# A chunk's sums are added to X by GpSimd, and the last output goes in two pieces

## The chip, the cores and the metric

The kernel runs on one core of a Trainium2 chip. A core has five engines with a queue each[...]: TensorE (PE in the profile, with its weight loads as PEld), VectorE (DVE), ScalarE (ACT), GpSimd (POOL) and SyncE (SP, which here only starts DMA transfers). The metric is the device time of one execution in microseconds (us), the median of several.

## The reference

A residual network of four layers on x of shape (4, 32, 32, 16): batch, height, width, channels. Each layer normalizes x by group norm (8 groups) and adds its result to x.

```python
def _L0_conv_ref(inputs, M, W, G):
    first = jnp.einsum('ijyx,byxc->bijc', Msq, inputs)
    kern = jnp.transpose(G, (0, 1, 5, 4, 2, 3)).reshape(h * w * f, c, G.shape[2], G.shape[3])
    shifted = lax.conv_general_dilated(x_nchw, kern, STRIDES, PADDING)
    ...
    diff = jax.nn.relu(inputs[:, None, None, :, :, :] - shifted)
    second = L * jnp.einsum('ijyx,bijyxc->bijc', Wsq, diff)
    return first - second

    x = x + _L0_conv_ref(_gn(x), L0_conv_M, L0_conv_W, L0_conv_G)
    x = x + _L1_conv_ref(_gn(x), L1_conv_M, L1_conv_W, L1_conv_G)
    x = x + _L2_conv_ref(_gn(x), L2_conv_W0, L2_conv_b0, L2_conv_W1, L2_conv_b1, L2_conv_W2, L2_conv_b2)
    x = x + _L3_conv_ref(_gn(x), L3_conv_M, L3_conv_Wp, L3_conv_G)
```

Layers 0, 1 and 3 are such convolutions. Each of the 1024 output positions has 3x3 filters of its own (G), which are applied to the whole image; the difference to the image, cut by a relu, is summed over the image with the weights W. Layer 2 is an interval layer: running maxima over intervals, then two steps with a maximum over split points and a sigmoid.

## The kernel before

The batch is cut in two groups g of two images. Three convolutions for two groups make six phases, in the order (g0, first), (g1, first), (g0, second), (g1, second), (g0, third), (g1, third), numbered 0 to 5. `X[g]` holds the group's x in SBUF as 128 partitions x 8 chunks x 32 (two images by 16 channels).

A phase runs over 8 chunks t of 128 output positions, a chunk over 32 steps (f, b): 16 channels by two images. A step is one bank pair of PSUM (`pc`, 128 x 1024), of which there are four. `first_part` (L588) writes products with the weights WU and WL and lets ScalarE scale the bank (L609); `second_part` (L612) adds the products with WD and W9, and VectorE then multiplies the bank, cut at zero, by the chunk's weights `WT` and sums it into one column of `acc` (L625, output `junk`, which nobody reads). TensorE runs one step ahead: the first part of a step is issued before the second part of the step in front of it. With the last of the 32 steps, VectorE adds the chunk's 32 sums, scaled by 1/EPS, to `X[g][:, t]` (L639). In the order of the instructions this stands behind the next chunk's first `first_part`.

Beside the steps two generators hand out small pieces of other work. `prep_parts` (L193) makes the weights: a unit is 4 channels of a chunk, 190 units in all are made here, one per 8 steps, two units ahead of their use. For a unit, VectorE cuts off the low bits (`upper`, L177), ScalarE makes W9, WD and WU (L153, L210, L213), GpSimd adds and subtracts (L223, twice L225, L187 for the next unit, twice L214), and then SP loads the raw weights of a later unit (`load_raw`, L98). `behind` (L670) prepares the next phase's images: group norm (L275), whose first sum (L279) reads all of `X[g]` of the group of the next phase, then transposes and DMAs through DRAM, then splitting of the images, on GpSimd too (L254, L261). In phases 3 and 4 it also computes the interval layer (L440): memsets (L453), a selection (L472), scans on VectorE (L483), products (L504, L517), and in two calls of `step` (L526) eight tables each on GpSimd (L536), each followed six steps later by a maximum over it on VectorE (L543).

All queues are in order: an instruction that waits for a semaphore holds all behind it on its engine. The schedule is the order in which the program is written; no scheduler moves anything. At the end SP writes `out[1]` from `X[1]` when the last chunk has been added (L841); `out[0]` went earlier, in phase 5 (L693).

Of the kernel before, what the change touches and what calls it, by code (L numbers as in the profile page):

```python
# [12 lines left out]
ALU = mybir.AluOpType  # L13
# [9 lines left out]
NT = NP // P  # L23
# [10 lines left out]
EPS = 2.0**-12  # L34
# [7 lines left out]
def net_kernel(ctx: ExitStack, tc: tile.TileContext, x, xq, xi, convs, iv_w, iv_b, out):  # L42
# [21 lines left out]
    nc = tc.nc  # L64
# [17 lines left out]
    phases = [(g, layer) for layer in range(NL) for g in range(NG)]  # L82
    n_chunks = len(phases) * NT

    X = [const.tile([P, NT, GC], F32, name=f"X{g}") for g in range(NG)]
# [487 lines left out]
    def products(ps, pairs, first):  # L573


        for k, (w, v) in enumerate(pairs):
            for h in range(2):
                r = slice(64 * h, 64 * h + 64)
                nc.tensor.matmul(  # L579
                    ps[:, h, :],  # L580
                    lhsT=w[r],
                    rhs=v[r],
                    start=first and k == 0,
                    stop=k == len(pairs) - 1,
                    skip_group_check=not first,
                )
# [25 lines left out]
    def second_part(step, ps):  # L612

        phase, t, f, b = step
        g = phases[phase][0]
        n = phase * NT + t
        u = n * NU + f // FU
        if u >= PLAIN:
            WU, WL, WD, W9 = (w[..., f % FU, :] for w in units[u])
            products(  # L620
                ps, [(WD[:, s], iyz[g][:, s, b]) for s in range(2)] + [(W9, im9[g][:, b])], False
            )
        col = b * C + f
        junk = work.tile([P, NP], F32, tag="junk", name=f"junk_{n}_{col}")
        nc.vector.scalar_tensor_tensor(  # L625
            junk,
            ps.rearrange("p h n -> p (h n)"),
            0.0,
            chunks[n],
            op0=ALU.min,  # L630
            op1=ALU.mult,
            accum_out=accs[phase][:, t, col : col + 1],
        )
        if (f, b) == (C - 1, GB - 1):
            acc = accs[phase][:, t]
            if n == 0:
                plain_acc = acc.rearrange("p (b c) -> p b c", c=C)[:, :, : PLAIN * FU]
                nc.vector.tensor_scalar_mul(plain_acc, plain_acc, EPS)
            nc.vector.scalar_tensor_tensor(  # L639
                X[g][:, t], acc, 1.0 / EPS, X[g][:, t], op0=ALU.mult, op1=ALU.add  # L640
            )

    accs = {}
    open_steps = []
# [1 line left out]
    def conv_layer(phase, behind):  # L646


        kind, wait = 1, 0
        accs[phase] = work.tile([P, NT, GC], F32, tag="acc", bufs=2, name=f"acc_{phase}")  # L650
        for t in range(NT):
            n = phase * NT + t
            steps = [(f, b) for f in range(C) for b in range(GB)]
            if n == 0:
                steps.sort(key=lambda s: (s[0] // FU, s[1]))
            for at, (f, b) in enumerate(steps):
                may = next(parts, (IDLE, CALM)) if n or at >= FIRST else (IDLE, CALM)
                if at == 4:
                    load_chunk(n + 1)
                step = (phase, t, f, b)  # L660
                open_steps.append((step, first_part(step)))
                if len(open_steps) > 1:
                    second_part(*open_steps.pop(0))
                wait -= 1
                if wait <= 0 and (kind > 0 or kind in may):
                    kind = wait = next(behind, 1 << 20)
        for _ in behind:
            pass
# [169 lines left out]
    for phase in range(len(phases)):  # L838
        conv_layer(phase, behind(phase))
    second_part(*open_steps.pop(0))  # L840
    nc.sync.dma_start(out[1], X[1])  # L841


# [74 lines left out]
```

## Time and profile before

| | us |
|---|---|
| median of 3 runs | 2578.73 (2576.74 to 2578.93) |
| the profiled execution | 2578.01 |
| its span | 2576.30 |
| L625 on VectorE, 1536 times | 1223 ns each |
| L214, L225, L223 on GpSimd, 950 times | 1303 to 1314 ns each |
| L639 on VectorE, 48 times | 24.3 in sum, 507 ns each in the mean |
| GpSimd idle before L223, waiting for ScalarE's W (L153) | 814.5 in sum, at most 13.0 |
| `out` from X, 128 KB, from issue to landing | 1.7 (the last) and 2.0 |

The profile is that of one execution. Lines of the order of time give the start in us from the span's start, the length in us, engine, line, operation, and the tiles written and read; in square brackets stands how long the engine was idle before it and what ended that. In the list of waits stand the sum, the number and the longest. Ends of matmuls are modelled, so TensorE's losses are better read from the spacing of starts. One step takes TensorE about 1.63 us, a chunk about 52.3.

### The profile page before, as it was taken

What the parts mean: (1) busy time and instruction counts of PE and PEld (TensorE: products, weight loads), DVE (VectorE), ACT (ScalarE), POOL (GpSimd) and SP (SyncE); (2) the same over time, 40 slices, a digit from 0 to 9 for tenths busy, and PEclk for the clock granted to TensorE, in tenths of its full rate; (3) what the DMA queues carried; (4) which work ended last, traced back from release to release, by engine and by line L of the source; (5) the groups of instructions that cost most, each with busy time, mean ns of one, the idle gap of its engine ahead of it and who ended that gap; (6) DMA issues with size and microseconds to landing.
All of it is one profiled execution on the core that took longest, in us unless ns stands there. A gap on an engine that the chain in (4) does not pass through costs nothing.

```text
span 2576.3 us, 56475 instructions
## 1 busy us (share of the span) xinstructions
PE 2558.4 (99%) x21906; PEld 2058.9 (80%) x21906; DVE 2150.0 (83%) x3651; ACT 2094.3 (81%) x2549; POOL 1565.7 (61%) x1289
## 2 busy tenths in 40 slices
PE   8999999999999999999999999999999999999999
PEld 5998788878888887888887877877778877788887
DVE  9888778888787887787789988889889887787777
ACT  4888788888888887888888888888888888788886
POOL 4667455575555556555566776576767676455553
PEclk9999999999999999999999999999999999999999
DMA  4424222242222432222222222322222234222220
GB/s 153 167 81 129 75 91 99 82 128 91 91 99 87 149 114 91 98 91 85 85 94 91 91 93 84 120 91 91 91 91 85 93 119 156 76 99 91 91 91 19
DMA packets 50284, 254.14 MB, mean 99 GB/s; under 512 B 12128, under 2 KB 14048, under 8 KB 24928
## 3 DMA queue, kind: packets, MB, share of 16 engines
q1 hardware_dynamic: 49056, 249.94, 28.9%
q8 instruction: 172, 2.82, 0.4%
q14 instruction: 96, 0.79, 0.1%
q10 hardware_dynamic: 832, 0.58, 0.1%
q0 software_dynamic: 128, 0.02, 0.0%
HBM read 248.99 MB, written 0.98 MB: 97 GB/s over the span
## 4 chain that ended last, share of the span: by engine, by line
PE 97%; DVE 2%; issue 1%; ACT 0%; DMA 0%; DVEq 0%; ACTq 0%
PE pc L579 96%; DVE junk L625 1%; PE pf L381 1%; ACT pc L609 0%; PE ps_l L504 0%; DMA XQ<-in_xq 0%; DVE s_a L543 0%; DVE s_b L543 0%; PE ps_r L517 0%; DVE X L639 0%; ACT L547 0%; ACT L319 0%; ACT s_a L547 0%; PE ps_y L565 0%; DVE raw L786 0%
## 5 line engine op out<-in xcount | busy, mean ns | idle before, releaser
L625 DVE SCALAR_TENSOR_TENSOR junk<-pc,WT 128x1024 f32<-128x1024 f32 x1536 | 1879.2, 1223 | 401.3 <-PE pc L579 351.3
L609 ACT ACTIVATE pc<-pc 128x1024 f32<-128x1024 f32 x1520 | 1531.6, 1008 | 445.6 <-PE pc L579 383.9
L579 PE MATMUL pc<-iy,WU 64*128 64x512 f32 x6080 | 967.5, 394 | 2.7 <-DVE junk L625 2.3
L579 PE MATMUL pc<-iyz,WD 64*128 64x512 f32 x6080 | 965.6, 393 | 3.0 <-ACT pc L609 3.0
L579 PE MATMUL pc<-iz,WL 64*128 64x512 f32 x6080 | 964.0, 392 | 0.0
L223 POOL TENSOR_TENSOR W<-W,raw 128x512 fp32r<-128x512 f32 x190 | 249.6, 1314 | 815.3 <-ACT W L153 814.5
L579 PEld LDWEIGHTS pc<-iy,WU 64*128 64x128 f32 x6080 | 579.7, 185 | 141.6 <-DVE junk L625 9.9
L579 PEld LDWEIGHTS pc<-iyz,WD 64*128 64x128 f32 x6080 | 580.9, 185 | 138.5 <-ACT pc L609 8.6
L579 PEld LDWEIGHTS pc<-iz,WL 64*128 64x128 f32 x6080 | 582.4, 185 | 129.7
L579 PE MATMUL pc<-im,W 64*128 64x512 f32 x3072 | 621.8, 397 | 0.0
L225 POOL TENSOR_TENSOR WL<-raw,upper_w 128x512 fp32r<-128x512 f32 x380 | 486.6, 1303 | 4.4 <-DVE upper_w L177 4.4
L214 POOL TENSOR_TENSOR WD<-WD,WL 128x512 fp32r<-128x512 f32 x380 | 488.4, 1309 | 0.1
L579 PEld LDWEIGHTS pc<-im,W 64*128 64x128 f32 x3072 | 294.5, 185 | 69.2 <-issue 3.4
L210 ACT ACTIVATE WD<-upper_w 128x512 fp32r<-128x512 f32 x380 | 236.8, 623 | 6.2 <-DVE upper_w L177 6.2
L213 ACT CAST WU<-upper_w 128x512 fp32r<-128x512 f32 x380 | 233.7, 615 | 0.9 <-issue 0.9
L187 POOL TENSOR_TENSOR raw<-raw,pick 128x512 f32<-128x512 f32 x190 | 202.3, 1065 | 8.7 <-DMA raw<-in_g 7.8
L177 DVE TENSOR_SCALAR upper_w<-raw 128x1024 int32<-128x1024 int32 x190 | 136.6, 719 | 0.1
L153 ACT ACTIVATE W<-raw,low_w 128x512 fp32r<-128x512 f32 x190 | 135.9, 715 | 0.1
L625 DVE DVE_READ_ACCUMULATOR junk<-pc,WT 128x1 f32 x1536 | 127.7, 83 | 0.0
L536 POOL TENSOR_TENSOR tables<-ft_b,rt 128x1089 f32<-128x1089 f32 x16 | 38.0, 2373 | 5.3 <-ACT ft_b L529 5.3
L536 POOL TENSOR_TENSOR tables<-ft_a,rt 128x1089 f32<-128x1089 f32 x16 | 37.9, 2366 | 4.6 <-ACT ft_a L529 4.6
L254 POOL TENSOR_TENSOR iz<-raw,upper_x 128x512 fp32r<-128x512 f32 x20 | 24.0, 1210 | 17.1 <-DVE upper_x L177 17.1
(134 smaller groups left out, 387.9 us busy)
## 6 DMA issues: line engine op xcount, KB each, us to landing
raw<-in_g SPq DMA_DIRECT2D x190, 1024.0 KB, 4.9
WT<-in_w SPq DMA_DIRECT2D x48, 512.0 KB, 3.5
MT<-in_mt SPq DMA_DIRECT2D x6, 2048.0 KB, 12.2
raw<-xs SPq DMA_DIRECT2D x120, 67.8 KB, 2.4
raw<-in_xi SPq DMA_DIRECT2D x3, 271.0 KB, 4.7
raw<-in_xi SPq DMA_DIRECT2D x1, 813.0 KB, 8.2
first<-in_g SPq DMA_DIRECT2D x1, 768.0 KB, 8.7
xs<-xt SPq DMA_DIRECT2D x20, 34.0 KB, 1.9
```

Of the source, the lines that this page charges most:

```text
L153: nc.scalar.activation(dst, src, AF.Copy, scale=mask[:, 1:2])
L177: nc.vector.tensor_scalar(t.bitcast(I32), src.bitcast(I32), HIGH, None, op0=ALU.bitwise_and)
L187: eng.tensor_tensor(raws[u][:, 1, at:to], raws[u][:, 1, at:to], pick[:, f0 + at : f0 + to].unsqueeze(2).to_broadcast([P, to - at, P]), ALU ...
L210: nc.scalar.activation(WD[:, s], high[:, s], AF.Copy, scale=-EPS)
L213: nc.scalar.copy(WU[:, s], high[:, s])
L214: nc.gpsimd.tensor_tensor(WD[:, s], WD.bitcast(F32)[:, s], WL.bitcast(F32)[:, s], ALU.add)
L223: nc.gpsimd.tensor_tensor(W9, W9.bitcast(F32), src[:, 3], ALU.add)
L225: nc.gpsimd.tensor_tensor(WL[:, s], w8[:, s], high[:, s], ALU.subtract)
L536: nc.gpsimd.tensor_tensor(t, ft[:, i, :].unsqueeze(1).to_broadcast([P, T1, T1]), rt, ALU.add,)
L579: nc.tensor.matmul(ps[:, h, :], lhsT=w[r], rhs=v[r], start=first and k == 0, stop=k == len(pairs) - 1, skip_group_check=not first,)
L609: nc.scalar.activation(ps, ps, AF.Copy, scale=1.0 + EPS)
L625: nc.vector.scalar_tensor_tensor(junk, ps.rearrange("p h n -> p (h n)"), 0.0, chunks[n], op0=ALU.min, op1=ALU.mult, accum_out=accs[phase][ ...
```

## The change

The scaled add of a chunk's sums (L639) is made by GpSimd in the first five phases, in two operations: `acc` is scaled in place, then added to X. In the last phase it stays on VectorE. There, with chunk 6 (`t == NT - 2`), SP is told to write the first seven chunks of `out[1]`, and the DMA at the end writes chunk 7 alone.

```diff
-            nc.vector.scalar_tensor_tensor(
-                X[g][:, t], acc, 1.0 / EPS, X[g][:, t], op0=ALU.mult, op1=ALU.add
-            )
+            if phase < len(phases) - 1:
+                nc.gpsimd.tensor_scalar_mul(acc, acc, 1.0 / EPS)
+                nc.gpsimd.tensor_tensor(X[g][:, t], X[g][:, t], acc, ALU.add)
+            else:
+                nc.vector.scalar_tensor_tensor(
+                    X[g][:, t], acc, 1.0 / EPS, X[g][:, t], op0=ALU.mult, op1=ALU.add
+                )
+                if t == NT - 2:
+                    nc.sync.dma_start(out[g][:, : NT - 1], X[g][:, : NT - 1])
...
     second_part(*open_steps.pop(0))
-    nc.sync.dma_start(out[1], X[1])
+    nc.sync.dma_start(out[1][:, NT - 1], X[1][:, NT - 1])
```

In the changed kernel the two GpSimd operations are L640 and L641, the add that stays on VectorE is L643, the new DMA L647 and the last one L847. Lines behind the change move down by six.

## The prediction

> **What bounds the kernel now.** I read the page first (engine shares, then the chain of work that ended last), then the rows of tile X, then TensorE, VectorE and GpSimd in order of time around the ends of chunks.
>
> ```profile
> PE 2558.4 (99%) x21906; PEld 2058.9 (80%) x21906; DVE 2150.0 (83%) x3651; ACT 2094.3 (81%) x2549; POOL 1565.7 (61%) x1289
> ...
> PE 97%; DVE 2%; issue 1%; ACT 0%; DMA 0%; DVEq 0%; ACTq 0%
> ```
>
> TensorE is busy 99% and carries 97% of the chain. Work taken from VectorE is worth something only where TensorE stood waiting for VectorE. The line that moves has this row in the view of tile X (durations in ns, min/median/max):
>
> ```profile
> L639 DVE SCALAR_TENSOR_TENSOR X<-acc,X x48: 191/193/2224, 71.9 to 2573.2; 128x32 f32<-128x32 f32 x48
> ```
>
> The add takes 0.19 us, but sometimes 2.2. Listing all 48, nine are over 0.6 us: eight of 1.5 to 2.2 in the phases that prepare the interval layer, and one of 0.87. VectorE in order of time at such a place (start us, length us):
>
> ```profile
> 1449.13 1.22 DVE L625 SCALAR_TENSOR_TENSOR junk<-pc,WT 128x1024 f32<-128x1024 f32 x1 [0.16 <-PE pc L579]
> 1450.28 0.08 DVE L625 DVE_READ_ACCUMULATOR junk<-pc,WT 128x1 f32 x1
> 1450.40 1.51 DVE L639 SCALAR_TENSOR_TENSOR X<-acc,X 128x32 f32<-128x32 f32 x1
> 1451.83 1.28 DVE L543 TENSOR_REDUCE s_a<-tables 128x33 f32<-128x1089 f32 x1
> 1453.02 1.21 DVE L625 SCALAR_TENSOR_TENSOR junk<-pc,WT 128x1024 f32<-128x1024 f32 x1
> 1454.16 0.08 DVE L625 DVE_READ_ACCUMULATOR junk<-pc,WT 128x1 f32 x1
> 1454.38 1.23 DVE L625 SCALAR_TENSOR_TENSOR junk<-pc,WT 128x1024 f32<-128x1024 f32 x1
> 1455.53 0.08 DVE L625 DVE_READ_ACCUMULATOR junk<-pc,WT 128x1 f32 x1
> 1455.53 1.31 DVE L177 TENSOR_SCALAR upper_w<-raw 128x1024 int32<-128x1024 int32 x1
> ```
>
> GpSimd in the same stretch:
>
> ```profile
> 1449.47 2.38 POOL L536 TENSOR_TENSOR tables<-ft_a,rt 128x1089 f32<-128x1089 f32 x1
> 1454.99 1.29 POOL L223 TENSOR_TENSOR W<-W,raw 128x512 fp32r<-128x512 f32 x1 [3.14 <-ACT W L153]
> ```
>
> The X add begins at 1450.40 and ends at 1451.91; GpSimd's L536 ends at 1451.85. The add was held until GpSimd was done. The same happens to upper_w at 1455.53 (1.31 instead of its mean 0.72) under L223. The reduce L543 and the junk lines keep their length beside GpSimd. TensorE pays:
>
> ```profile
> 1451.90 0.41 PE L579 MATMUL pc<-im,W 64*128 64x512 f32 x2
> 1452.14 0.64 PE L579 MATMUL pc<-iy,WU 64*128 64x512 f32 x4
> ...
> 1453.54 0.40 PE L579 MATMUL pc<-im,W 64*128 64x512 f32 x2
> 1454.30 0.73 PE L579 MATMUL pc<-iy,WU 64*128 64x512 f32 x4 [0.36 <-DVE junk L625]
> 1454.87 0.63 PE L579 MATMUL pc<-iz,WL 64*128 64x512 f32 x4
> ...
> 1457.43 0.40 PE L579 MATMUL pc<-im,W 64*128 64x512 f32 x2
> 1458.03 0.73 PE L579 MATMUL pc<-iy,WU 64*128 64x512 f32 x4 [0.20 <-DVE junk L625]
> 1458.60 0.63 PE L579 MATMUL pc<-iz,WL 64*128 64x512 f32 x4
> ```
>
> By starts: an x2 group is normally followed after 0.24 us (1451.90 to 1452.14), an x4 group after 0.46. Here the steps are 0.76 and 0.57, then 0.60 and 0.57: lost 0.53 + 0.10 + 0.37 + 0.10, that is 1.09 us with rounding, more than the gaps in brackets. The starts at 1562, 1883 and 1991 us give 1.09, 1.09 and 1.10: 4.37 us in four places, chunks 2 and 4 of phases 3 and 4. At the other four long adds (1397, 1506, 1826, 1935) the same reading gives no loss: TensorE had just spent time on the interval layer's own products.
>
> **What the Trainium skill says.** "SBUF — State Buffer", Who interferes with whom: VectorE with two SBUF inputs, or in a 2-port mode, and a GpSimd operation that reads SBUF exclude each other for a whole instruction; tensor_reduce never contends. The trace agrees with each part (1.51, 1.31, 1.28 us above). "Perfetto Trace Analysis", GPSIMD Engine Instruction: GpSimd spans are unreliable, so time by starts. I do: in the trace four 64x32 operations (L415) take 0.84 us together, 0.21 each. "DMA: Bandwidth & Descriptors", Anatomy of one DMA: most of a transfer's fixed time is the receipt of the write. In the trace the last output's packets move for 0.52 us of the 1.71 from issue to landing, which agrees.
>
> **The change part by part.**
>
> *Out of VectorE: 40 adds.* A free add costs nothing even where VectorE has a backlog: junk follows junk after 1.37 us without the add, and after 1.38 with it (1343.29 to 1344.67). The 32 adds off the eight places therefore give 0. At the four paying places, s_a goes right behind the junk, at 1450.28 instead of 1451.83. The next junk then ends at about 1452.7, where TensorE would want its bank at about 1453.77 (0.23 after its start at 1453.54). Slack 1 us. The third junk, now after an upper_w at about 1454.0 (before L223 starts at 1455.0), ends near 1456.1 and is wanted at about 1457.0. Both stalls should go: -4.37. If upper_w is held once more, the second stall stays: 4 x 0.47 = 1.9 less gain.
>
> *Into GpSimd: 80 operations of 128x32.* Nearest rows: L307, 128x16, after which the dependent L309 starts 0.33 later, and L415, 0.21 to 0.25. A pair takes 0.33 + 0.25 = 0.58; bounds 0.45 and 1.2. The built order puts each pair directly before the first GpSimd instruction that stood behind the chunk's end. That instruction is usually L223 of the next unit, which starts 4.62 us after the chunk's last junk ends (445.98 to 450.61) because it waits for ScalarE's W. GpSimd ended its previous L214 at 444.85, so the pair's wait for the junk (1.1 us) and the pair itself lie in 5.76 us of idle: 0. Where the next one is L261, L453 or L536 (13 places) GpSimd now waits 0.1 to 1.2 us for the junk and that instruction starts 0.7 to 1.9 us later. The next L223 still has over 1 us of cover; the tables are read by a reduce only in the next interval step, six steps of 1.63 us later. Cost 0. L536 then lies at 1451.0 to 1453.4, beside a reduce and junk lines, which it doesn't hold.
>
> *New wait: the group norm's first sum (L279) for GpSimd.* At the start of phases 1 and 2 it stands right behind the chunk's last junk (446.25). It now waits for the pair: 0.08 + 0.58 + 0.05 after 445.98, so about 446.7, 0.45 us late. Behind it stands the next junk, and behind that TensorE's bank. The bank is wanted 4.64 us after the last junk's start (1449.13 to 1453.77), here 449.39; junk would end at 448.25. Cover 1.1 us: cost 0. In phases 3 and 4 the sum stands one junk later (1291.99 against 1290.44): no wait. X's other readers come later on GpSimd itself.
>
> *The output.* Seven eighths leave after chunk 6 of the last phase, at about 2521.4. On SP's queue this DMA stands ahead of the last raw load (issued at 2516.58 before). That load now waits for the add at 2521.24, goes at about 2521.9 and lands after 4.8 us at 2526.7; its first reader is L187 at 2529.58. Cover 2.9 us: 0. The last piece has 128 packets of 128 bytes instead of 1024. Packets of 1024 took 46 ns, of 136 bytes 12 ns (xs), eight per engine: 8 x 34 = 0.27 us off at best; but the first of each four xs transfers, 34 KB in small packets, landed after 1.6 to 1.9, against 1.71. Bounds 0.35 gain, 0.2 loss; I take a gain of 0.15.
>
> **Sum.** -4.37 - 0.15 = -4.5 us on the profiled execution's 2578.01 (span 2576.30): 2573.5. The four executions shown average 2578.1, so I don't move it to the median of 2578.73.
>
> **Rivals.**
> - *Half the gain.* The second stall stays, since upper_w meets L223 or the later L536: 2578.0 - 2.5 - 0.15 = 2575.3. For: upper_w was held at 1455.53. Against: it now comes about 1 us before L223.
> - *No gain.* VectorE stays late at the four places, for instance because s_a starts no earlier: 2577.9. Against: its table was made six steps earlier.
> - *Slower.* One mechanism: the pair is long, and the sum L279 at the starts of phases 1 and 2 holds the junk and TensorE. From a pair of 1.65 us on it costs its excess twice; beyond about 2 us L536 reaches upper_w and the four stalls are back too. Past +0.2% from a pair of about 4.2 us; at 4.4, 2 x 2.75: 2583.5. For: GpSimd's spans are rough. Against: the starts (0.21, 0.33).
> - *More.* The interval phases have other waits of TensorE for junk (1384 and 1813, 0.37 each; 1367 and 1796, 0.2 each). If some of that went too: 2572.4. Against: at those places VectorE is filled by the scans L483, and a free add costs it 0.01.
>
> **How the numbers follow.** Chances: forecast 0.66, half 0.13, none 0.07, slower 0.07, more 0.07. 0.2% of the median is 5.2 us, about what a measurement of this kernel tells from no change; the bound lies at 2573.6, in the middle of the forecast's own spread (2572.3 to 2574.7, from the output's bounds and the spread of the runs, 2.2 us). About two thirds of the forecast's chance falls below it, as its upper bounds on cost all have cover: with "more", 0.50 faster. The rest, half and none give 0.43 the same; slower 0.07. The range 2571.5 to 2577.0 holds the forecast, half and more, and leaves out slower and most of none.
>
> **What would show it.** Right: no bracketed wait of TensorE for junk near 1454, 1458, 1562, 1566, 1883, 1887, 1991 and 1995 us (shifted), s_a 1.15 us behind the junk before it, and L640 and L641 together under 0.7 us, inside GpSimd's idle before L223. Wrong: a row of L279 waiting for L641 over 1 us, upper_w above 1 us at those places, or a last output that lands later than 1.9 us.

## The result, and the profile after

| | before | after |
|---|---|---|
| median of 22 runs each, us | 2578.64 (2576.74 to 2579.70) | 2574.24 (2572.94 to 2575.89) |
| the profiled execution, us | 2578.01 | 2573.84 |
| its span, us | 2576.3 | 2572.1 |

The ratio is 0.9984, with a 95% interval from 0.9978 to 0.9990. The changed kernel is 4.4 us faster; the forecast had -4.5. That is 0.17%, just under what was set as the bound of no change, and the interval lies on both sides of it.

The page of the kernel after, busy time by engine and the chain that ended last:

```profile
PE 2556.7 (99%) x21906; PEld 2059.4 (80%) x21906; DVE 2128.6 (83%) x3611; ACT 2094.1 (81%) x2549; POOL 1586.0 (62%) x1369
...
PE 98%; DVE 1%; issue 1%; ACT 0%; DMA 0%; DVEq 0%
```

VectorE has lost 40 instructions and 21 us, GpSimd has gained 80 and 20 us, and the time follows neither: TensorE still carries 98% of the chain, pairs of its matmuls start every 233 ns as before, and so the time can only have changed in its gaps. The two new rows, in the view of tile acc (ns, min/median/max):

```profile
L640 POOL TENSOR_SCALAR acc<-acc x40: 287/288/293, 72.0 to 2144.5; 128x32 f32<-128x32 f32 x40
L641 POOL TENSOR_TENSOR X<-X,acc x40: 250/252/256, 72.4 to 2144.9; 128x32 f32<-128x32 f32 x40
```

Neither is ever long. The same place as was shown of before, VectorE in order of time (the second fence is GpSimd):

```profile
1448.59 1.22 DVE L625 SCALAR_TENSOR_TENSOR junk<-pc,WT 128x1024 f32<-128x1024 f32 x1 [0.16 <-PE pc L579]
...
1449.74 1.28 DVE L543 TENSOR_REDUCE s_a<-tables 128x33 f32<-128x1089 f32 x1
1450.94 1.21 DVE L625 SCALAR_TENSOR_TENSOR junk<-pc,WT 128x1024 f32<-128x1024 f32 x1
...
1453.44 0.69 DVE L177 TENSOR_SCALAR upper_w<-raw 128x1024 int32<-128x1024 int32 x1
```

```profile
1449.91 0.29 POOL L640 TENSOR_SCALAR acc<-acc 128x32 f32<-128x32 f32 x1 [0.90 <-DVE junk L625]
1450.28 0.25 POOL L641 TENSOR_TENSOR X<-X,acc 128x32 f32<-128x32 f32 x1
1450.49 2.37 POOL L536 TENSOR_TENSOR tables<-ft_a,rt 128x1089 f32<-128x1089 f32 x1
1454.45 1.30 POOL L223 TENSOR_TENSOR W<-W,raw 128x512 fp32r<-128x512 f32 x1 [1.59 <-ACT W L153]
```

The reduce s_a now follows the junk after 1.15 us (1448.59 to 1449.74), and L536 beside it holds nothing on VectorE. upper_w is done before L223 starts and takes 0.69 us. TensorE has no gap in this stretch, nor at the three other places. Seen over the whole span, its losses at the ends of chunks were 1.09, 1.09, 1.09 and 1.10 us and are now none.

But there is a loss that was not in the kernel before. VectorE, GpSimd and TensorE of the kernel after around 1551.8 us:

```profile
1546.51 1.23 DVE L625 SCALAR_TENSOR_TENSOR junk<-pc,WT 128x1024 f32<-128x1024 f32 x1 [0.75 <-ACT pc L609]
...
1547.65 1.28 DVE L543 TENSOR_REDUCE s_b<-tables 128x33 f32<-128x1089 f32 x1
1548.85 1.73 DVE L177 TENSOR_SCALAR upper_w<-raw 128x1024 int32<-128x1024 int32 x1
```

```profile
1548.74 1.28 POOL L223 TENSOR_TENSOR W<-W,raw 128x512 fp32r<-128x512 f32 x1 [3.42 <-ACT W L153]
```

```profile
1550.56 0.39 PE L579 MATMUL pc<-im,W 64*128 64x512 f32 x2
1551.78 0.73 PE L579 MATMUL pc<-iy,WU 64*128 64x512 f32 x4 [0.83 <-DVE junk L625]
```

L223 starts 0.11 us ahead of upper_w, so upper_w takes 1.73 us, and TensorE's next group comes after 1.22 us instead of 0.24: with the step behind it 1.09 us are lost. It is the old collision, at a place where it had not been: in the kernel before upper_w starts there at 1550.13, 0.24 us ahead of L223, and takes 0.68.

The sum over the two profiled executions: four places -4.37, the new loss +1.09, the landing of the last output -0.28 (1.71 to 1.43 us), and -0.66 at 111 us, where ScalarE took 1.52 us over issuing the small DMA of `bv` (L404) in the kernel before and 0.45 in this one. That makes -4.22; measured were -4.17. The 0.66 is not counted as the change's: of the twelve profiles of the experiments six have the long issue, and e3 below, whose instructions up to that point are those of before, has the short one.

### The profile page after: what moved, and what is told of

It reads as the page before. It is cut to its first block, busy times and chain, and to the rows that moved or that the text cites. A ratio compares the mean times of both kernels' runs of the same rounds, so it can differ in the third digit from the quotient of the medians.

```text
span 2572.1 us, 56552 instructions
## 1 busy us (share of the span) xinstructions
PE 2556.7 (99%) x21906; PEld 2059.4 (80%) x21906; DVE 2128.6 (83%) x3611; ACT 2094.1 (81%) x2549; POOL 1586.0 (62%) x1369
## 4 chain that ended last, share of the span: by engine, by line
PE 98%; DVE 1%; issue 1%; ACT 0%; DMA 0%; DVEq 0%
PE pc L579 97%; PE pf L381 1%; DVE junk L625 0%; ACT pc L609 0%; PE ps_l L504 0%; DMA XQ<-in_xq 0%; PE ps_r L517 0%; DVE upper_w L177 0%; ACT L319 0%; ACT L547 0%; ACT s_a L547 0%; PE ps_y L565 0%; DVE raw L792 0%; ACT rstd_c L319 0%; PE ps_v L743 0%
## 5 line engine op out<-in xcount | busy, mean ns | idle before, releaser
L223 POOL TENSOR_TENSOR W<-W,raw 128x512 fp32r<-128x512 f32 x190 | 249.3, 1312 | 766.3 <-ACT W L153 765.8
L225 POOL TENSOR_TENSOR WL<-raw,upper_w 128x512 fp32r<-128x512 f32 x380 | 486.5, 1303 | 2.6 <-DVE upper_w L177 2.6
L187 POOL TENSOR_TENSOR raw<-raw,pick 128x512 f32<-128x512 f32 x190 | 202.3, 1065 | 6.9 <-DMA raw<-in_g 6.9
L640 POOL TENSOR_SCALAR acc<-acc 128x32 f32<-128x32 f32 x40 | 11.5, 288 | 54.4 <-DVE junk L625 52.9
L536 POOL TENSOR_TENSOR tables<-ft_b,rt 128x1089 f32<-128x1089 f32 x16 | 38.0, 2373 | 0.0
L536 POOL TENSOR_TENSOR tables<-ft_a,rt 128x1089 f32<-128x1089 f32 x16 | 37.9, 2367 | 0.0
```

Source lines behind the costliest of these rows:

```text
L187: eng.tensor_tensor(raws[u][:, 1, at:to], raws[u][:, 1, at:to], pick[:, f0 + at : f0 + to].unsqueeze(2).to_broadcast([P, to - at, P]), ALU ...
L223: nc.gpsimd.tensor_tensor(W9, W9.bitcast(F32), src[:, 3], ALU.add)
L225: nc.gpsimd.tensor_tensor(WL[:, s], w8[:, s], high[:, s], ALU.subtract)
L536: nc.gpsimd.tensor_tensor(t, ft[:, i, :].unsqueeze(1).to_broadcast([P, T1, T1]), rt, ALU.add,)
```

## The experiments

Each was compared with runs of the kernel before on the same chip, whose medians were 2577.94 to 2578.48 us.

**The two parts alone.** e1 makes the adds on GpSimd as in the changed kernel, but writes the output in one piece; e2 the reverse.

```diff
# e1_add_only, against the changed kernel
-                if t == NT - 2:
-                    nc.sync.dma_start(out[g][:, : NT - 1], X[g][:, : NT - 1])
...
-    nc.sync.dma_start(out[1][:, NT - 1], X[1][:, NT - 1])
+    nc.sync.dma_start(out[1], X[1])
# e2_output_only, against the kernel before
+            if phase == len(phases) - 1 and t == NT - 2:
+                nc.sync.dma_start(out[g][:, : NT - 1], X[g][:, : NT - 1])
...
-    nc.sync.dma_start(out[1], X[1])
+    nc.sync.dma_start(out[1][:, NT - 1], X[1][:, NT - 1])
```

> The two GpSimd operations as in the change, but the last output in one piece as before. Forecast's theory: the stalls of TensorE at the four paying places go (4.4 us), the output is worth 0.15 to 0.3: 4.1 to 4.4 us under the kernel before. Rival 'the gain is spread over all chunks or comes from the output': under 3 us. The profile should show no wait of TensorE for junk at the four places, each X add on GpSimd, and the last output landing after 1.7 us.

> The add stays on VectorE everywhere, only the last output goes in two pieces. Theory: the last piece lands 0.28 us sooner (1.43 against 1.71): 0.15 to 0.3 us under the kernel before, the four places with their 1.09 us each as before. Rival (much of the gain is the output): 1 us or more under it.

e1: 2574.72 us, ratio 0.9987 (0.9981 to 0.9994), that is -3.5, less than the 4.1 to 4.4 expected; the four stalls are gone, but the loss near 1552, which no theory had, is there (1.09), and the output lands after 1.71 us. e2: 2577.84 us, ratio 0.9999 (0.9991 to 1.0007); the four stalls are 1.09 to 1.11 us each, the output lands after 1.43. So the gain is that of the adds. The output's 0.28 us is in both traces that have the two pieces, but too small for the runs to show.

**Which adds.** e3 moves only the adds of chunks 2 and 4 in phases 3 and 4, e4 only the 36 others. Both leave the output in one piece.

```diff
# against the changed kernel
-            if phase < len(phases) - 1:
# e3_four_places
+            if phase in (3, 4) and t in (2, 4):
# e4_other_places
+            if phase < len(phases) - 1 and not (phase in (3, 4) and t in (2, 4)):
```

> GpSimd makes the add only at chunks 2 and 4 of phases 3 and 4; the other 44 adds stay on VectorE; output in one piece. Theory: all of the gain is there, so the same as with all 40 on GpSimd: about 4.2 us under the kernel before. Rival 'VectorE's time is what counts' (40 adds of 0.19 us and the long ones): a tenth of it, 0.4 us.

> The counterpart: GpSimd makes the 36 other adds, VectorE those four; output in one piece. Theory: 0 within 0.5 us of the kernel before, the four stalls of 1.09 us still there. Rival 'VectorE's time is what counts': 3 us or more under it, since four of the eight long adds (2.1 us each) and all the short ones are gone from VectorE.

e3: 2573.76 us, ratio 0.9982 (0.9975 to 0.9989), -4.5; e4: 2578.22 us, ratio 1.0 (0.9992 to 1.0008). Four adds bring the whole gain, and 36 bring nothing in sum. e3 even does without the loss near 1552, and is 1.0 us under e1. e4 keeps the stalls at three of the four places; at the fourth its X add takes 0.50 us, because the loss of 1.09 us now comes 9 us earlier, at 1553.7, and the add starts at 1560.51, shortly before L536 ends at 1560.96. Ahead of that loss upper_w takes 1.73 us, as in the kernel after.

e3 also says where the new loss is from. VectorE in e3, same step as was shown of after:

```profile
1543.64 1.23 DVE L625 SCALAR_TENSOR_TENSOR junk<-pc,WT 128x1024 f32<-128x1024 f32 x1 [0.57 <-ACT pc L609]
...
1548.89 0.68 DVE L177 TENSOR_SCALAR upper_w<-raw 128x1024 int32<-128x1024 int32 x1
```

GpSimd in e3:

```profile
1549.13 1.61 POOL L223 TENSOR_TENSOR W<-W,raw 128x512 fp32r<-128x512 f32 x1 [3.41 <-ACT W L153]
```

In every trace VectorE starts some instructions late: counted from 0 through its queue with its waits for semaphores, those whose number leaves 63 when divided by 128. In the kernel after sixteen such are junk lines: fifteen start 0.40 us after the wait for the semaphore in front of them has ended, one after 0.76; ten of the twelve lines of the next number that have such a wait start after 0.04. The late start costs nothing where VectorE has time in hand. In both kernels here it is the record numbered 3263. In e3, as in the kernel before, that is the junk at 1543.64, and two more junk lines follow in which to catch up before s_b and upper_w. In the kernel after it is the junk at 1546.51, directly ahead of s_b and upper_w. Had it started 0.36 us earlier, upper_w would have come at about 1548.5, ahead of L223 (an estimate from the lines above). Up to this point the queue of the changed kernel has lost 28 adds and three waits for semaphores and gained 25 such waits, six records net; that of e3 has lost one add and gained one wait. The six records have moved the late start to another junk.

The other traces agree. e1, e4, e10, e11 and e6 with three operations have it at the same junk, and upper_w takes 1.70 to 1.73 us there; in e5 one junk lies between, and upper_w takes 0.68. But no run moves the late start alone, so this cause is argued from traces, and e9 below shows the same collision without a late start ahead of it. What VectorE does in those 0.36 us the profile doesn't tell.

**Is it GpSimd's doing the add, or VectorE's not doing it there?** e5 uses neither: VectorE adds all eight chunks of a phase at once, at the phase's end (128x256 instead of eight times 128x32; in the last phase chunk by chunk, as before).

```diff
-            nc.vector.scalar_tensor_tensor(
-                X[g][:, t], acc, 1.0 / EPS, X[g][:, t], op0=ALU.mult, op1=ALU.add
-            )
+            if phase == len(phases) - 1 or t == NT - 1:
+                s = slice(t, t + 1) if phase == len(phases) - 1 else slice(0, NT)
+                nc.vector.scalar_tensor_tensor(
+                    X[g][:, s], accs[phase][:, s], 1.0 / EPS, X[g][:, s], op0=ALU.mult, op1=ALU.add
+                )
```

> No add on GpSimd: VectorE adds all eight chunks' sums in one operation of 128x256 at the end of each of the first five phases (the last phase and the output as before). Theory (what helped is that no add with two SBUF inputs stands before s_a on VectorE[...], not GpSimd's help): the four stalls go, 4.2 us under the kernel before. Rival 'the work had to go to GpSimd': no gain.

2573.90 us, ratio 0.9984 (0.9977 to 0.9990). No stall at the four places and none near 1552. The gain is that VectorE has no add behind the junk there; that GpSimd makes it instead is not needed.

**How long may the pair be?** e6_pair_plus_3 and e6_pair_plus_8 put so many more GpSimd operations of 128x32 between the two, which write a tile nobody reads.

```diff
                 nc.gpsimd.tensor_scalar_mul(acc, acc, 1.0 / EPS)
+                for _ in range(8):
+                    nc.gpsimd.tensor_scalar_mul(spare, acc, 1.0)
...
+    spare = const.tile([P, GC], F32, name="spare")
```

> The change, with three more 128x32 operations on GpSimd between the scaling and the add (into a tile nobody reads), 0.37 us each from start to start: the pair takes about 1.75 us instead of 0.64. Theory of the covers: the sum L279 at the starts of phases 1 and 2 may wait for a pair of 1.65 us, so 0.1 us twice; at the four places L536 ends about 1454.0 and holds upper_w for 0.5 us, within its cover: 0 to 0.5 us over the change. Rival 'GpSimd has no cover at a chunk's end': 40 x 1.1 = 44 us over it.

> The same with eight more operations: the pair takes about 3.6 us. Theory of the covers: 2 x (3.6 - 1.65) = 3.9 us at the starts of phases 1 and 2, and at the four places L536 now ends at about 1455.9, upper_w is held for over 2 us and TensorE waits again, 0.9 us four times: about 7.5 us over the change, so 3 us over the kernel before. Rival 'GpSimd has no cover at a chunk's end': 40 x 3 = 120 us over the change. Rival 'cover everywhere': no change.

The times were a surprise: 2539.15 us with three (ratio 0.9849, 0.9836 to 0.9863) and 2555.98 with eight (0.9915, 0.9902 to 0.9929), both far faster than with none. The new tile does that, not the operations; see below. The kernel to compare them with is therefore e10 below, the changed kernel with an unused tile of the same size: three operations cost 5.2 us over its 2533.96 and eight cost 22.0, where 0 to 0.5 and about 7.5 were expected.

By the starts of matmuls against e10's: with three, the sum L279 at the starts of phases 1 and 2 waits 1.7 us for the pair, which costs TensorE 0.15 us at once and then more, since upper_w comes behind L223 (1.81 us): 1.5 at each of the two starts, 0.7 at each of three further places (near 236, 550 and 961 us), and nothing at the four places. With eight it waits 3.6 us, and 2.0 us are lost at the starts of phases 1 and 2 (expected 1.95), 1.3 to 1.55 at the four places (expected 0.9). Where I had expected none, 2.1 us are lost at the starts of phases 3 and 4, 1.9 some 60 us after them, and 1.1 to 1.2 some 26 us after each of the four places. The mechanism of the rival "slower" exists, where it said, from about the length it said; it decides nothing at 0.62 us. Its price was too low.

**The other half of the collision.** Does upper_w meet L223 by accident of order? e8 is the kernel before with L223 behind the two L225 of the same unit.

```diff
-            nc.gpsimd.tensor_tensor(W9, W9.bitcast(F32), src[:, 3], ALU.add)
             for s in range(2):
                 nc.gpsimd.tensor_tensor(WL[:, s], w8[:, s], high[:, s], ALU.subtract)
+            nc.gpsimd.tensor_tensor(W9, W9.bitcast(F32), src[:, 3], ALU.add)
```

> The kernel before with one reordering on GpSimd: the addition to W9 (L223) goes behind the two subtractions (L225), which wait for VectorE's upper_w, so that L223 can no longer hold upper_w. Theory: the second stall at the four places (0.47 us) was upper_w under L223 and goes, the first (0.63 us) stays: 1.9 us under the kernel before. Rival (both stalls are one backlog of VectorE from the held add): no gain.

2576.96 us, ratio 0.9997 (0.9988 to 1.0005): 1.3 us less, with an interval that includes no change. VectorE in e8:

```profile
1450.30 1.80 DVE L639 SCALAR_TENSOR_TENSOR X<-acc,X 128x32 f32<-128x32 f32 x1
...
1455.72 0.69 DVE L177 TENSOR_SCALAR upper_w<-raw 128x1024 int32<-128x1024 int32 x1
```

At this first place upper_w takes 0.69 us and the second stall is gone, as expected. But GpSimd runs later, L536 ends at 1452.05 instead of 1451.85, and the X add is held for 1.80 us instead of 1.51: the first stall grew from 0.63 to 0.92. That leaves 0.17 us at each of the four places, 0.7 in all, not the 1.9 expected. The two stalls had one sort of cause, two operations of GpSimd, and this order of GpSimd's work mostly trades one for the other.

**The tile.** e9 is the kernel before with an unused tile of 128 bytes a partition, allocated ahead of the weights' buffers; no instruction is added or removed. e10 is the changed kernel with it, e11 with one of 64 bytes.

```diff
+    const.tile([P, 32], F32, name="spare")
     accs = {}
# e11_after_pad_64
+    const.tile([P, 16], F32, name="spare")
```

> The kernel before with one tile more in SBUF that nothing reads or writes, 128 bytes a partition, standing ahead of the weights' buffers; no instruction differs. The run with three more GpSimd operations was 39 us faster, with a matmul pair every 229 ns instead of 233; it also had such a tile. Theory 'addresses': the weights' buffers stand 128 bytes further, and that alone sets the pace: about 2578 - 39 + 2 = 2541 us or a few more, pair spacing 229 ns. Rival 'the additional GpSimd operations did it': 2578 us, 233 ns.

> The change with the same unused tile of 128 bytes. Theory 'addresses': 229 ns a pair and, since a step of TensorE is then 0.03 us shorter and VectorE's covers with it, the change is worth as much as before or a little more against the kernel before with the tile: 4.4 to 6 us. Against the run with three more GpSimd operations: 2.3 us or so faster, what that one lost at the starts of phases 1 and 2 in its profile (1.13 and 1.14). Rival: 2574 us.

> The change with an unused tile of 64 bytes, by which the weights' buffers start at multiples of 512 bytes (their slices of 512 bytes too). Theory 'slices that cross a boundary cost TensorE': as fast as with 128 bytes or faster, 229 ns a pair or less. Rival 'only the distance to the images' addresses counts, or nothing simple': 233 ns or more.

| | us | ratio to before (95%) | ns between pairs of matmuls |
|---|---|---|---|
| e9, before + 128 bytes | 2540.92 | 0.9857 (0.9844 to 0.9871) | 229 |
| e10, after + 128 bytes | 2533.96 | 0.9828 (0.9815 to 0.9842) | 229 |
| e11, after + 64 bytes | 2569.71 | 0.9967 (0.9955 to 0.9980) | 232 |

These are medians over the span; before and after have 233. TensorE in e9, away from any stall; iy to iy is one step:

```profile
700.15 0.62 PE L579 MATMUL pc<-iy,WU 64*128 64x512 f32 x4
...
701.75 0.62 PE L579 MATMUL pc<-iy,WU 64*128 64x512 f32 x4
```

A step takes 1.60 us instead of 1.63 in the kernel before (699.76 to 701.40, in the same view), a chunk 51.27 instead of 52.27. Over 48 chunks that would be 48 us; e9 gives part of it back, among it 4.7 us at the four further places named below. The tile stands ahead of the weights' buffers, so that they and all that is allocated behind them move by 128 bytes; the images' buffers, allocated earlier, stay. If the tile of e11 puts the weights' buffers on multiples of 512 bytes, as its expectation has it (no trace shows addresses), they start 448 bytes into such a line in before and 64 in e9. The theory of e11, that slices which cross a boundary make the pace slow, then fails, since its pace is 232.

Nor is it the address alone. With the tile and the same buffers, TensorE falls back to 233 ns for long stretches: in e9 from 121 to 224 and from 1379 to 1431 us, in e10 from 1376 to 1468 and from 1911 to 2004. By these paces such a stretch costs 1.8% of its length, about 1.6 us in 92. What in the address counts, and what switches the pace within one execution, stays open.

The change is worth more with the tile: 7.0 us between the medians of e9 and e10, 8.9 between their spans, of which 0.75 are the long issue of `bv` in e9. The four places cost 1.1 to 1.2 us each in e9, and so do four further ones (1463.6, 1571.6, 1888.4 and 1996.3 us). At these upper_w takes 1.77 to 1.79 us because L223 starts 0.05 to 0.08 ahead of it; VectorE and GpSimd ahead of the first of them:

```profile
1460.64 1.79 DVE L177 TENSOR_SCALAR upper_w<-raw 128x1024 int32<-128x1024 int32 x1
```

```profile
1460.60 1.29 POOL L223 TENSOR_TENSOR W<-W,raw 128x512 fp32r<-128x512 f32 x1 [5.52 <-ACT W L153]
```

No late start stands among the three junk lines ahead of any of the four. e10 has none of these eight and one other, 1.17 at 1527.5, where upper_w takes 1.72 us: it is the record 3263 and the step of the new loss again.

**The best version.** e12 is e10 with L223 behind the two L225, to rid it of that loss.

> The changed kernel with the unused tile of 128 bytes a partition, and GpSimd's conversion of W (L223) moved behind the two L225 of the same chunk. Theory 'the one loss left in that kernel, 1.17 us at 1527.5, is upper_w held by L223 and goes when L223 starts later': no loss there, upper_w at some 0.69 us everywhere, and about 1.2 us under the 2533.96 of the kernel with the tile alone, 2532.8. Rival 'the later L223 costs as much elsewhere, as in the kernel before, where the first of the two stalls grew by 0.3 us': new losses of about 1 us in all at boundaries of chunks, and 2534 or more. Less than 2531 would be against both.

2530.51 us (2528.81 to 2535.19), ratio 0.9817 (0.9804 to 0.9831). The loss is gone: at that step upper_w takes 0.68 us (at 1522.90), where e10 has 1.72. But the whole is 3.4 us under e10 between the medians, and below the 2531 that would speak against both theories; the single runs of the two overlap (e10: 2531.51 to 2535.09). In the profiled executions e12 is 4.0 us shorter. By the starts of matmuls, 1.05 of that are at that place, 2.8 lie where e10 falls back to 233 ns for two stretches and e12 for one (1841 to 1902), 0.5 near 1343 and 0.3 near 1762; the rest goes either way. So the loss at 1527.5 went as the theory says, and the larger part is the pace; whether the order of GpSimd's work has to do with that isn't shown. It is the fastest kernel measured here, by 48 us under before, of which the tile brings 37 to 40.

## Why the prediction was right

The forecast was 2573.5 us, measured were 2574.2, and the gain came where and how it said. By its steps:

- *Four places pay, -4.37.* Shown: e3, with these four adds alone, gives -4.5, and no stall is left at any of them.
- *The 32 other free adds and the four other long ones give 0.* Shown by e4: no change. What the step missed is that an instruction that costs nothing can still, by being gone, shift what stands behind it.
- *upper_w comes before L223 at the four places.* Right there: 1453.44 against 1454.45. The rival "half the gain" named the right mechanism, upper_w held by L223, and the wrong place: it struck once, at 1548.85, at a step of chunk 4 in phase 3 ahead of the chunk's end, for 1.09 us, with VectorE's late start at the junk ahead of it. This is the term that the sum lacked: 2573.5 and 1.09 make 2574.6.
- *The reduce keeps its length beside GpSimd.* True, but the reduce of 1.28 us quoted for it doesn't show it: L536 ended at 1451.85, just as that reduce began (1451.83). The trace of before shows it elsewhere: at 1420.88 a reduce takes 1.28 us with L536 (1420.54 to 1422.89) beside it all the way. In the kernel after, the reduces at the four places run beside the pair and L536, and take 1.28 to 1.29.
- *The pair takes 0.58 us.* 0.37 from start to start and 0.25, that is 0.62. It lies in idle time before L223: that is 3.91 us at 450.03 even with the pair in front of it.
- *L279 is 0.45 us late at the starts of phases 1 and 2, at no cost.* It starts 1.98 us after the start of the chunk's last junk (444.17 to 446.15), before 1.50 (444.75 to 446.25): 0.48 late, and TensorE loses nothing there. Its row in the list of waits of the kernel after (us in total, times, longest):

```profile
DVE part L279 <- POOL X L641: 1.5, 2, 0.7
```

  Two waits, none over 0.75 us. e6 shows the cover: with three more operations, 1.61 us from the pair's start to its end, TensorE loses 0.15 at once, so the limit of 1.65 us was about right. The second price behind it, upper_w meeting L223 once VectorE is late, was not in the working.
- *L261, L453 and L536 later at 13 places, at no cost.* L536 lies at 1450.49 to 1452.86, and no new gap of TensorE stands at these places.
- *The output, -0.15, bounds +0.35 gain and 0.2 loss.* -0.28, inside, and close to the 0.27 that the working gave as the best case. In both kernels the first packet moves 0.84 us after the issue and the landing comes 0.35 after the last packet; between them lie 0.52 us before and 0.23 after. The Trainium skill, "DMA: Bandwidth & Descriptors", Specifications, gives 512 bytes as the least transfer for full rate; the trace agrees, with 13 ns for a packet of 128 bytes and 46 for one of 1024, but with an eighth of the data this DMA still landed sooner. The raw load behind the larger piece went at 2518.2, landed after 5.9 us instead of 4.8, and kept 1.8 of the 2.9 us of cover: its reader L187 starts at 2525.9 without a wait for it.
- *The total.* That the profiled execution has 2573.84 against 2573.5 is luck: the new loss of 1.09 was made up by 0.66 at `bv`, which isn't counted as the change's, and by 0.13 more at the output.

## What to carry to other kernels

Before moving work to another engine, look which few of its executions cost the bottleneck anything, and ask at each what holds it: here four of 40 adds made the whole gain, each held behind a GpSimd operation, and not doing them at that point (one add a phase) did as well as moving them. An instruction that costs nothing can still decide where the next collision falls; after removing some, read the stretches in which VectorE and GpSimd come within a few tenths of a microsecond of each other. And when a control with an added tile is much faster than it should be, run the tile alone: here that was worth eight to nine times the change.

## What the hardware did that I had not expected

- An unused tile of 128 bytes a partition ahead of the weights' buffers made matmul pairs start every 229 ns instead of 233, and the kernel 37 us faster (e9); 64 bytes gave 232. In e9, e10 and e12, with the tile, it fell back to 233 for 50 to 100 us at a time.
- In all fourteen traces VectorE starts one record in 128 of its queue some 0.36 us late, read on junk lines (0.40 after the wait has ended, instead of 0.04).
- The issue of one DMA of 1.5 KB by ScalarE (`bv`, L404) took 0.44 us in seven of the profiled executions and 1.5 to 1.9 in the other seven, in before and e3 with the same instructions up to it.
- upper_w and L223 collided at a step where the prediction expected nothing. The Trainium skill, "SBUF — State Buffer", Who interferes with whom, counts tensor_scalar among the operations that can take the port pair shared with GpSimd and so be held for a whole instruction. The trace agrees: in the kernel after upper_w took 1.73 us with L223 0.11 us ahead of it, and 0.69 where it was 1.0 us ahead of L223.
